# Attention weights transposed by VectorE and DRAM, with TensorE's and the transfers' order fixed by a timetable, in a two-layer graph kernel

## The chip, the cores and the metric

One core of one Trainium2 chip. Times are device microseconds (us) of the whole kernel, all in float32. A kernel is timed beside the kernel before on the same chip in alternating rounds. "The kernel before" took 3456.9 us (median of 4 runs in the rounds with the change, 3453.3 to 3458.0).

## The reference, cut to what matters

There are 128 graphs of 128 nodes with 256 features, and a dense integer adjacency (values 0 and 1) per graph. Layer 0 is two rounds of graph attention, a residual, a layer norm and a feed-forward block. Layer 1 is attention with 8 heads whose weights are masked by relation before they meet the values:

```python
# layer 0, twice:
e = leaky_relu(Wh1 + swapaxes(Wh2, 1, 2)); att = softmax(where(adj > 0, e, NEG), axis=1); h = att @ Wh
# layer 1:
attn = softmax(q @ k.T / sqrt(dh))                       # 8 heads, 128 x 128 each
for r in range(4):
    out += (attn * (adj == r)) @ (src @ Wv[r] + bv[r])   # needs attn with the nodes j on partitions
x = ln(src + out @ Wo + bo); x = ln(x + gelu(x @ W1) @ W2)
```

The last matmul contracts over `j`, so the attention weights, which come out of the softmax with `i` on partitions, have to be transposed: 8 blocks of 128x128 per graph, 1024 in all.

## The kernel before

It works on groups of four graphs, 32 groups, in five stages (load, graph attention, feed-forward 0, attention, feed-forward 1) that overlap between groups. The parts that the change touches:

```python
def transposed(y, direct):                 # of activations: VectorE turns 32x32 blocks, DRAM moves them
    ...
    nc.vector.transpose(z, y)
    for i in range(NQ):                    # four writes of 128 KB, runs of 128 bytes
        nc.sync.dma_start(s[:, :, i]..., z[ts(i, Q)]...)
    nc.sync.dma_start(t, s...)             # one read of 512 KB

def gat_weighting(wh, c, cap, direct):     # graph attention's weights
    nc.vector.transpose(z, wh[:, :, c + 1:c + 2].to_broadcast([P, G, Q]))
    nc.sync.dma_start(s..., z[::Q])        # the row transfer: 2 KB out ...
    nc.sync.dma_start(p, ...)              # ... and 256 KB back, the same row on all partitions
    # ScalarE, VectorE, ScalarE, GpSimd -> att

def by_relation(b, es):                    # attention: TensorE transposes, VectorE masks from PSUM
    for e in es:
        pT = ps.tile([P, HC, N], F32, name="tr", bufs=2)
        for q in range(HC):
            nc.tensor.transpose(pT[:, q], e[:, q], ident)                             # line 369
        for r in range(R):
            nc.vector.scalar_tensor_tensor(m, ab, r, pT, op0=OP.is_equal, op1=OP.mult)  # line 373
...
with tile.TileContext(nc, schedule_with_timeline_sim=True) as tc:
```

The stages are generators; a heap steps them by a virtual time, which sets priorities. The final order of every engine's instructions, and of the transfers in the one issuing queue, comes from a simulated timeline. It is fixed when the kernel is built.

Of the kernel before, what the change touches and what calls it, by code (L numbers as in the profile page):

```python
# [23 lines left out]
G = 4  # L24
Q = 32
# [14 lines left out]
def graph_layers(ctx: ExitStack, tc: tile.TileContext, a: dict, out: bass.AP):  # L40
# [21 lines left out]
    TB, KB = 4, 6  # L62
# [6 lines left out]
    ps = ctx.enter_context(tc.tile_pool(name="ps", bufs=5, space=PSUM))  # L69
# [69 lines left out]
    plus = wk.tile([P, 3, D], F32, name="plus", tag="T", bufs=TB)  # L139
# [72 lines left out]
    def transposed(y, direct):  # L212

        t = wk.tile([P, G, DC, N], F32, name="T", bufs=TB)
        if direct:
            for c in range(DC):
                p = ps.tile([P, G, N], F32, name="tr", bufs=2)
                for b in range(G):
                    nc.tensor.transpose(p[:, b], y[:, b, ts(c, P)], ident)
                if c % 2:  # L220
                    nc.vector.tensor_copy(t[:, :, c], p)
                else:
                    nc.scalar.copy(t[:, :, c], p)
            return t
        z = wk.tile([P, G, D // Q, Q], F32, name="z", bufs=1)
        nc.vector.transpose(z, y)  # L226
        s = dr.tile([G, D, NQ, Q], F32, name="zd")
        for i in range(NQ):
            nc.sync.dma_start(s[:, :, i].rearrange("b (j a) t -> a (b j) t", a=Q),
                              z[ts(i, Q)].rearrange("a b j t -> a (b j) t"))  # L230
        nc.sync.dma_start(t, s.rearrange("b (c p) i t -> p b c (i t)", p=P))
        return t

    def feed_forward(y, before, direct, win, bin_, wout, func, by=G):


        hT = transposed(y, direct)
        yield 2
        fT = []
        for f0 in range(0, FC, 2):  # L240
# [8 lines left out]
            yield 1  # L249
            if f0 in (2, 4):  # L250
                affine(y, before, f0 - 2)
        for b2_ in range(0, G, 2):
# [5 lines left out]
            yield 2  # L258
# [4 lines left out]
    def gat_weighting(wh, c, cap, direct):  # L263

        e = wk.tile([P, G, N], F32, name="e")
        if direct:
            p = ps.tile([P, G, N], F32, name="tr", bufs=2)
            for b in range(G):
                nc.tensor.transpose(p[:, b], wh[:, b, c + 1:c + 2].to_broadcast([P, N]), ident)
        else:  # L270
# [4 lines left out]
            p = wk.tile([P, G, N], F32, name="row", bufs=1)  # L275
# [13 lines left out]
    def gat_block(direct, xg, xt, at):  # L289
# [3 lines left out]
        wh = wk.tile([P, G, MW], F32, name="wh", tag="wh", bufs=1)  # L293
        for b in range(G):
# [4 lines left out]
            if b % 2:  # L299
                yield 1  # L300
        att = gat_weighting(wh, D + 2, cap, direct)
        yield 6
        wh2 = wk.tile([P, G, D + 2], F32, name="wh2", bufs=1)
        for b in range(G):
            p = ps.tile([P, D + 2], F32, name="mm")
            nc.tensor.matmul(p, att[:, b], wh[:, b, :D + 2], start=True, stop=True)  # L306
            nc.scalar.copy(wh2[:, b], p)
        yield 1
        att = gat_weighting(wh2, D, cap, direct)
        yield 6  # L310
        y = xg
        for b2_ in range(0, G, 2):
            p = ps.tile([P, 2, D], F32, name="mm")
            for b in (b2_, b2_ + 1):
                nc.tensor.matmul(p[:, b - b2_], att[:, b], wh2[:, b, :D], start=True, stop=True)  # L315
# [4 lines left out]
    def attention(y, at, direct):  # L320

        hT = transposed(y, direct)
        yield 2
        qT = wk.tile([P, DC, T], F32, name="T", bufs=TB)
# [13 lines left out]

        def weights(b):
# [8 lines left out]
            es = []  # L348
            for p in scores:
# [4 lines left out]
                e = wk.tile([P, HC, N], F32, name="e1", bufs=4)  # L354
                for q in range(HC):
                    nc.scalar.activation(e[:, q], p[:, q], AF.Exp, bias=nm[:, q:q + 1], accum_out=s[:, q:q + 1])  # L356
                nc.vector.reciprocal(s, s)  # L357
                nc.gpsimd.tensor_mul(e, e, per_row(s, N))  # L358
                es.append(e)
            return es  # L360

        def by_relation(b, es):

            ab = at[:, b][:, None, :].to_broadcast([P, HC, N])
            ms = []
            for e in es:
                pT = ps.tile([P, HC, N], F32, name="tr", bufs=2)
                for q in range(HC):
                    nc.tensor.transpose(pT[:, q], e[:, q], ident)  # L369
                ms.append([])  # L370
                for r in range(R):
                    m = wk.tile([P, HC, N], F32, name="m", bufs=DC * R)
                    nc.vector.scalar_tensor_tensor(m, ab, r, pT, op0=OP.is_equal, op1=OP.mult)  # L373
# [27 lines left out]
        yield 1  # L401
        es = [weights(0)]
        yield 1
        es.append(weights(1))
        yield 1
        for b in range(G):
# [3 lines left out]
            v = values(b)  # L410
            yield 1.5

            with tc.high_priority(offset=200):
                oT, last = weighted(ms, v)
                if b + 2 < G:
                    with tc.issue_after(last.ins):
                        es.append(weights(b + 2))
            yield 1.5
# [3 lines left out]
            nc.vector.tensor_add(y[:, b], y[:, b], p)  # L422
        normalised(y)
# [19 lines left out]
    def stage_gat(g):  # L443
        x0[g], masks[g] = yield from gat_block(g < 2, *loads.pop(g))
# [8 lines left out]
    def stage_attention(g):  # L453
# [5 lines left out]
        x2[g] = yield from attention(x1.pop(g), masks.pop(g), alone(g))  # L459

    def stage_ff1(g):
# [6 lines left out]
        if not last:  # L468
            nc.sync.dma_start(out[g], y)

    stages = ((stage_load, 1, -0.8, -0.7000000000000001), (stage_gat, 15, -0.1, 0.45), (stage_ff0, 9, 0.7, 1.2),
              (stage_attention, 17, 1.7, 3), (stage_ff1, 9, 3.2, 3.7))
    todo = []
    for g in range(NG):
        for n, (stage, total, begin, end) in enumerate(stages):
            if g == 1 and n == 1:
                begin, end = begin - 0.6, end - 0.6
            todo.append([g + begin, n, g, stage(g), (end - begin) / total])
    heapq.heapify(todo)
    while todo:  # L480
        t, n, g, steps, each = heapq.heappop(todo)
        try:
            share = next(steps)
        except StopIteration:
# [52 lines left out]
```

## Time and profile before

| | kernel before |
|---|---|
| time | 3456.9 us |
| TensorE busy | 98% of the span, 95% of the chain that ended last |
| other engines | at most 51% (ScalarE) |
| DMA | 20.8% of 16 engines |
| distance of line 306 in successive groups ("the period") | 104.0 us |

The period is read from start times in the trace: the mean over 20 groups in the middle. The middle of the kernel, 1000 to 2800 us, is the place to look. In the view of stretches the columns are the stretch, its length, then busy time and number of instructions of TensorE, its weight load, VectorE, ScalarE and GpSimd, then the granted clock (of TensorE; 1.00 is full speed), the DMA's share and GB/s. Line numbers are those of each kernel's own file: line 319 of the changed kernel is 306 before, and 321 in the runs that hold the masks back. Of before:

```profile
1000.00:2800.00 1800.00, 1800.00 (x10514) 1170.61 (x10513) 892.03 (x1944) 954.79 (x2530) 640.00 (x732) 1.00 0.23 54
```

TensorE has no idle time here. (Some matmul records are missing from any trace, so counts between traces are not compared.)

### The profile page before, as it was taken

The page shows a single profiled execution, that of the slowest core. Times are in us where ns is not written, and L with a number is a line of the kernel's source. Part 1 is how long each engine was busy: PE and PEld are TensorE (multiplying, and loading weights), DVE is VectorE, ACT ScalarE, POOL GpSimd, SP SyncE. Part 2 cuts the span into 40 slices and gives each one's busy share as a digit, 9 for nine tenths or more (in the row PEclk, how much of TensorE's full clock was granted, in tenths as well). Part 3 has the DMA queues.
Part 4 walks back from the last instruction along what each step waited for, and adds up shares of the span by engine and source line. Part 5 has one row for each costly group of instructions (what it writes and reads, how often), then busy time and mean ns, then how long its engine had stood idle before and what let it go on. Part 6 is the DMA issues. An engine that isn't in the chain of part 4 may idle for free.

```text
span 3451.6 us, 51872 instructions
## 1 busy us (share of the span) xinstructions
PE 3381.2 (98%) x19624; PEld 2197.9 (64%) x19624; DVE 1655.4 (48%) x3605; ACT 1763.8 (51%) x4724; POOL 1176.5 (34%) x1352
## 2 busy tenths in 40 slices
PE   7999999999999999999999999999999999999987
PEld 5656666666666666666666666666666666666655
DVE  2544454544454544454444454444454444554443
ACT  3444555645545645546545556545556545556332
POOL 2233343233333333333333333333333333333332
PEclk9999999999999999999999999999999999999999
DMA  5012222122222122221222221222221222221000
GB/s 188 13 41 55 57 47 55 47 65 51 60 47 52 50 62 53 56 52 47 55 62 53 56 53 44 59 62 53 56 53 42 60 62 53 49 44 38 19 19 13
DMA packets 501769, 181.10 MB, mean 52 GB/s; under 512 B 380432, under 2 KB 476176, under 8 KB 501392
## 3 DMA queue, kind: packets, MB, share of 16 engines
q1 hardware_dynamic: 501520, 177.79, 20.8%
q8 instruction: 155, 2.54, 0.3%
q14 instruction: 94, 0.77, 0.1%
HBM read 113.66 MB, written 64.09 MB: 51 GB/s over the span
## 4 chain that ended last, share of the span: by engine, by line
PE 95%; DVE 2%; ACT 1%; DMA 1%; POOL 0%; SPq 0%; issue 0%; ACTq 0%; DVEq 0%; POOLq 0%
PE mm L256 26%; PE mm L244 26%; PE mm L382 12%; PE av L394 7%; PE mm L346 5%; PE mm L297 4%; PE tr L369 3%; PE mm L334 3%; PE mm L328 3%; PE mm L421 3%; PE mm L306 2%; PE mm L315 2%; DVE m L373 1%; PE mm L172 0%; DMA zd<-z 0%; DMA wf<-in_wf_dram 0%
## 5 line engine op out<-in xcount | busy, mean ns | idle before, releaser
L210 POOL TENSOR_TENSOR tok<-tok,ln_rows 128x512 f32<-128x512 f32 x508 | 630.4, 1273 | 334.1 <-DVE z L226 172.8
L358 POOL TENSOR_TENSOR e<-e,s 128x512 f32<-128x512 f32 x256 | 266.3, 1041 | 1209.3 <-DVE s L357 983.3
L373 DVE SCALAR_TENSOR_TENSOR m<-at,tr 128x512 f32<-128x512 int32 x1024 | 629.6, 680 | 99.5 <-PE av L394 64.0
L247 ACT ACTIVATE fT<-mm,col 128x512 f32<-128x512 f32 x512 | 342.9, 691 | 415.1 <-PE mm L244 412.8
L244 PE MATMUL mm<-T,w 128*128 128x512 f32 x1024 | 471.6, 599 | 7.3 <-DMA T<-zd 5.4
L244 PE MATMUL mm<-T,wf 128*128 128x512 f32 x1024 | 466.5, 599 | 5.3 <-DMA T<-zd 3.7
L256 PE MATMUL mm<-w,fT 128*128 128x256 f32 x2048 | 470.6, 381 | 0.0
L382 PE MATMUL mm<-wv,T 128*128 128x512 f32 x1024 | 467.5, 594 | 0.0
L256 PE MATMUL mm<-wf,fT 128*128 128x256 f32 x2048 | 453.4, 379 | 0.0
L256 PEld LDWEIGHTS mm<-w,fT 128*128 128x128 f32 x2048 | 386.5, 190 | 97.9 <-issue 44.6
L256 PEld LDWEIGHTS mm<-wf,fT 128*128 128x128 f32 x2048 | 388.1, 191 | 66.2 <-issue 16.5
L352 DVE TENSOR_REDUCE nm<-mm 128x4 f32<-128x512 f32 x256 | 166.2, 681 | 541.8 <-PE mm L346 541.8
L204 ACT ACTIVATE tok<-tok,nmr,rstd 128x256 f32<-128x256 f32 x512 | 268.7, 590 | 259.8 <-POOL nmr L202 250.8
L398 ACT COPY oT<-av 128x256 f32<-128x256 f32 x128 | 47.9, 374 | 673.9 <-PE av L394 673.2
L356 ACT ACTIVATE e<-mm,nm 128x128 f32<-128x128 f32 x1024 | 359.8, 372 | 18.1 <-DVE nm L352 16.6
L244 PEld LDWEIGHTS mm<-T,wf 128*128 128x128 f32 x1024 | 196.3, 192 | 225.8 <-issue 209.2
L244 PEld LDWEIGHTS mm<-T,w 128*128 128x128 f32 x1024 | 188.1, 191 | 208.1 <-issue 190.3
L382 PEld LDWEIGHTS mm<-wv,T 128*128 128x128 f32 x1024 | 192.4, 191 | 176.1 <-issue 166.4
L394 PEld LDWEIGHTS av<-m,v 128*32 128x32 f32 x8192 | 217.1, 110 | 72.8 <-issue 44.6
L394 PE MATMUL av<-m,v 128*32 128x128 f32 x8192 | 251.8, 275 | 10.0 <-DVE v L383 8.8
L257 DVE TENSOR_TENSOR tok<-tok,mm 128x512 f32<-128x512 f32 x128 | 86.6, 676 | 319.8 <-PE mm L256 309.1
L337 ACT ACTIVATE kbd<-mm,col 32x512 f32<-32x512 f32 x256 | 173.9, 679 | 85.6 <-PE mm L334 83.0
(84 smaller groups left out, 3667.7 us busy)
## 6 DMA issues: line engine op xcount, KB each, us to landing
zd<-z SPq DMA_DIRECT2D x360, 128.0 KB
T<-zd SPq DMA_DIRECT2D x90, 512.0 KB
xt<-in_xT_dram SPq DMA_DIRECT2D x32, 512.0 KB
tok<-in_x_dram SPq DMA_DIRECT2D x32, 512.0 KB
out_dram<-tok SPq DMA_DIRECT2D x31, 512.0 KB
row<-zsd SPq DMA_DIRECT2D x60, 256.0 KB
at<-in_adjT_dram SPq DMA_DIRECT2D x32, 256.0 KB
wf<-in_wf_dram SPq DMA_DIRECT2D x2, 1024.0 KB
```

What stands on the lines that cost most here:

```text
L204: nc.scalar.activation(y[:, b], y[:, b], AF.Identity, bias=nmr[:, b:b + 1], scale=rstd[:, b:b + 1])
L210: engine.tensor_tensor(y[:, b:b + 2], y[:, b:b + 2], v[:, None, :].to_broadcast([P, 2, D]), op)
L244: nc.tensor.matmul(p, win[:, c, ts(f0 + i, P)], hT[:, :, c], start=c == 0, stop=c == DC - 1)
L247: nc.scalar.activation(t, p, func, bias=bin_[:, f0 + i:f0 + i + 1])
L256: nc.tensor.matmul(p[:, b - b2_], fT[f][:, ts(b, N)], wout[:, f], start=f == 0, stop=f == FC - 1)
L337: nc.scalar.activation(kbd[c][rows, :, q % 2], p[rows], AF.Identity, bias=bk[rows, c:c + 1])
L346: nc.tensor.matmul(scores[h][:, c], qT[rows, c, ts(b, N)], kbd[c][rows, b], start=True, stop=True, tile_position=(h * P // 2, 0))
L356: nc.scalar.activation(e[:, q], p[:, q], AF.Exp, bias=nm[:, q:q + 1], accum_out=s[:, q:q + 1])
L358: nc.gpsimd.tensor_mul(e, e, per_row(s, N))
L373: nc.vector.scalar_tensor_tensor(m, ab, r, pT, op0=OP.is_equal, op1=OP.mult)
L382: nc.tensor.matmul(p, hT[:, b, f], wv[:, f, r:r + 2], start=f == 0, stop=f == DC - 1)
L394: last = nc.tensor.matmul(po[ts(q, DH), c], v[:, r, c * P + q * DH:c * P + (q + 1) * DH], ms[q // 2][r][:, c * 2 + q % 2], start=r == R - ...
```

## The change

Two things. First, the attention weights of 31 of the 32 groups are transposed as activations already were: VectorE turns blocks in place, four writes to DRAM and a read put them together (`eT`). That is meant to free TensorE. Second, latency is planned by a timetable in units of about a microsecond per stage step, 100 units per group, and TensorE and the issuing queue (SP) are made to keep the order in which the program emits instructions. VectorE, ScalarE and GpSimd still get theirs from the simulated timeline. Smaller things come with it: one more PSUM bank for matmuls (in this program, the piece of memory that matmuls write a result into and that another engine reads before it is used again), a copy of the adjacency into PSUM, the values of a graph computed one step ahead, and no raised priority any more for the small matmuls with the attention weights.

```diff
+KEPT = {mybir.EngineType.PE: (250, 3150), mybir.EngineType.SP: (0, 4000)}
...
-    ps = ctx.enter_context(tc.tile_pool(name="ps", bufs=5, space=PSUM))
+    ps = ctx.enter_context(tc.tile_pool(name="ps", bufs=6, space=PSUM))
...  (gat_weighting: steps of the stage, in units)
-        yield 6
+        yield 29
...  (attention)
+        adj = ps.tile([P, G, N], F32, name="adj", bufs=1)
+        nc.vector.tensor_copy(adj, at)
...
-            return es
+            return e if direct else turned(e)
+        def turned(e):
+            eT = wk.tile([P, H, N], F32, name="eT")
+            transposed(e, eT, direct, over=True)
+            return eT
...  (by_relation)
-                pT = ps.tile([P, HC, N], F32, name="tr", bufs=2)
-                for q in range(HC):
-                    nc.tensor.transpose(pT[:, q], e[:, q], ident)
-                    nc.vector.scalar_tensor_tensor(m, ab, r, pT, op0=OP.is_equal, op1=OP.mult)
+                    nc.vector.scalar_tensor_tensor(m, ab, r, eT[:, ts(h, HC)], op0=OP.is_equal, op1=OP.mult)
...
+    stages = (stage_load, -75), (stage_gat, -31), (stage_ff0, 40), (stage_attention, 125), (stage_ff1, 290)
...  (for every new instruction i of an engine in KEPT)
+                tc.add_manual_dep(i, last[i.engine], ... NoSync ..., reason="order of emission")
```

More of the change, by code (lines that the diff above doesn't have):

```diff
@@ L24 @@
 G = 4
+LEAD = 35
+EARLY = {(1, 1): 70, (1,2): 50, (2,0): 80, (2,1): 90, (2,2): 90}
+KEPT = {mybir.EngineType.PE: (250, 3150), mybir.EngineType.SP: (0, 4000)}
 Q = 32
@@ L61, in graph_layers @@
     HC = P // DH
-    TB, KB = 4, 6
+    TB, KB = 5, 6
     SCALE = 1.0 / float(np.sqrt(DH))
@@ L138, in graph_layers @@
     nc.sync.dma_start(ln_rows, on_all_rows(0, 8))
-    plus = wk.tile([P, 3, D], F32, name="plus", tag="T", bufs=TB)
+    plus = wk.tile([P, G * MW], F32, name="plus", tag="T", bufs=TB)[:, :3 * D].rearrange("p (k d) -> p k d", k=3)
     nc.sync.dma_start(plus, on_all_rows(8, 3))
@@ L210, in affine, with transposed, t_tile, features @@
             engine.tensor_tensor(y[:, b:b + 2], y[:, b:b + 2], v[:, None, :].to_broadcast([P, 2, D]), op)
-    def transposed(y, direct):
-        t = wk.tile([P, G, DC, N], F32, name="T", bufs=TB)
+    def transposed(y, t, direct, over=False):
+        n = y.shape[1]
         if direct:
-            for c in range(DC):
-                p = ps.tile([P, G, N], F32, name="tr", bufs=2)
+            for k in range(0, n, G):
+                p = ps.tile([P, G, N], F32, name="mm")
                 for b in range(G):
-                    nc.tensor.transpose(p[:, b], y[:, b, ts(c, P)], ident)
-                if c % 2:
-                    nc.vector.tensor_copy(t[:, :, c], p)
-                else:
-                    nc.scalar.copy(t[:, :, c], p)
-            return t
-        z = wk.tile([P, G, D // Q, Q], F32, name="z", bufs=1)
+                    nc.tensor.transpose(p[:, b], y[:, k + b], ident)
+                if k:
+                    nc.vector.tensor_copy(t[:, k:k + G], p)
+                else:
+                    nc.scalar.copy(t[:, k:k + G], p)
+            return
+        z = y if over else wk.tile([P, n, N], F32, name="z", bufs=1)
         nc.vector.transpose(z, y)
-        s = dr.tile([G, D, NQ, Q], F32, name="zd")
+        s = dr.tile([n, N, NQ, Q], F32, name="zd", bufs=8)
         for i in range(NQ):
-            nc.sync.dma_start(s[:, :, i].rearrange("b (j a) t -> a (b j) t", a=Q),
-                              z[ts(i, Q)].rearrange("a b j t -> a (b j) t"))
-        nc.sync.dma_start(t, s.rearrange("b (c p) i t -> p b c (i t)", p=P))
+            nc.sync.dma_start(s[:, :, i].rearrange("k (j a) t -> a (k j) t", a=Q),
+                              z[ts(i, Q)].rearrange("a k (j t) -> a (k j) t", t=Q))
+        nc.sync.dma_start(t, s.rearrange("k p i t -> p k (i t)"))
+    def t_tile():
+        return wk.tile([P, G * MW], F32, name="T", bufs=TB)[:, :G * D]
+    def features(y, direct):
+        t = t_tile().rearrange("p (b c n) -> p b c n", b=G, c=DC)
+        transposed(y.rearrange("p b (c f) -> p (b c) f", f=P), t.rearrange("p b c n -> p (b c) n"), direct)
         return t
     def feed_forward(y, before, direct, win, bin_, wout, func, by=G):
-        hT = transposed(y, direct)
-        yield 2
+        hT = features(y, direct)
+        yield LEAD
         fT = []
@@ L248, in feed_forward @@
                 fT.append(t)
-            yield 1
+            yield 6
             if f0 in (2, 4):
@@ L257, in feed_forward @@
             nc.vector.tensor_add(y[:, b2_:b2_ + 2], y[:, b2_:b2_ + 2], p)
-            yield 2
+            yield 12.5
             if (b2_ + 2) % by == 0:
@@ L266, in gat_weighting @@
         if direct:
-            p = ps.tile([P, G, N], F32, name="tr", bufs=2)
+            p = ps.tile([P, G, N], F32, name="mm")
             for b in range(G):
@@ L274, in gat_weighting @@
             nc.sync.dma_start(s.rearrange("b i t -> i b t"), z[::Q])
-            p = wk.tile([P, G, N], F32, name="row", bufs=1)
+            p = e
             nc.sync.dma_start(p, bass.AP(tensor=s.tensor, offset=s.offset, ap=[[0, P], [1, G * N]]))
@@ L287, in gat_weighting, with gat_block @@
         return e
-    def gat_block(direct, xg, xt, at):
+    def gat_block(direct, tag, xg, xt, at):
         cap = wk.tile([P, G, N], F32, name="cap")
         nc.vector.tensor_scalar(cap, at, 0, 2 * BIG, op0=OP.is_gt, op1=OP.mult)
-        wh = wk.tile([P, G, MW], F32, name="wh", tag="wh", bufs=1)
+        wh = wk.tile([P, G, MW], F32, name="wh", tag=tag, bufs=TB if tag == "T" else 1)
         for b in range(G):
@@ L299, in gat_block @@
             if b % 2:
-                yield 1
+                yield 3
         att = gat_weighting(wh, D + 2, cap, direct)
-        yield 6
-        wh2 = wk.tile([P, G, D + 2], F32, name="wh2", bufs=1)
+        yield 29
         for b in range(G):
@@ L306, in gat_block @@
             nc.tensor.matmul(p, att[:, b], wh[:, b, :D + 2], start=True, stop=True)
-            nc.scalar.copy(wh2[:, b], p)
-        yield 1
-        att = gat_weighting(wh2, D, cap, direct)
-        yield 6
+            nc.scalar.copy(wh[:, b, :D + 2], p)
+        yield 2
+        att = gat_weighting(wh, D, cap, direct)
+        yield 29
         y = xg
@@ L314, in gat_block @@
             for b in (b2_, b2_ + 1):
-                nc.tensor.matmul(p[:, b - b2_], att[:, b], wh2[:, b, :D], start=True, stop=True)
+                nc.tensor.matmul(p[:, b - b2_], att[:, b], wh[:, b, :D], start=True, stop=True)
             nc.vector.tensor_add(y[:, b2_:b2_ + 2], xg[:, b2_:b2_ + 2], p)
@@ L318, in gat_block, with attention @@
         return y, at
-    def attention(y, at, direct):
-        hT = transposed(y, direct)
-        yield 2
-        qT = wk.tile([P, DC, T], F32, name="T", bufs=TB)
+    def attention(y, at, first, direct):
+        hT = features(y, first or direct)
+        yield LEAD
+        qT = t_tile().rearrange("p (c t) -> p c t", c=DC)
         for c in range(DC):
@@ L347, in weights @@
                                      start=True, stop=True, tile_position=(h * P // 2, 0))
-            es = []
-            for p in scores:
+            e = wk.tile([P, H, N], F32, name="e1")
+            for h, p in enumerate(scores):
                 p = p.rearrange("p c q n -> p (c q) n")
@@ L353, in weights, with by_relation @@
                 s = sm.tile([P, HC], F32, name="s1")
-                e = wk.tile([P, HC, N], F32, name="e1", bufs=4)
+                eh = e[:, ts(h, HC)]
                 for q in range(HC):
-                    nc.scalar.activation(e[:, q], p[:, q], AF.Exp, bias=nm[:, q:q + 1], accum_out=s[:, q:q + 1])
+                    nc.scalar.activation(eh[:, q], p[:, q], AF.Exp, bias=nm[:, q:q + 1], accum_out=s[:, q:q + 1])
                 nc.vector.reciprocal(s, s)
-                nc.gpsimd.tensor_mul(e, e, per_row(s, N))
-                es.append(e)
-            return es
-        def by_relation(b, es):
-            ab = at[:, b][:, None, :].to_broadcast([P, HC, N])
+                nc.gpsimd.tensor_mul(eh, eh, per_row(s, N))
+            return e if direct else turned(e)
[3 more added lines that the diff above has]
+            return eT
+        def by_relation(b, eT):
+            if direct:
+                eT = turned(eT)
+            ab = adj[:, b][:, None, :].to_broadcast([P, HC, N])
             ms = []
-            for e in es:
-                pT = ps.tile([P, HC, N], F32, name="tr", bufs=2)
-                for q in range(HC):
-                    nc.tensor.transpose(pT[:, q], e[:, q], ident)
+            for h in range(2):
                 ms.append([])
@@ L399, in weighted @@
             return oT, last
-        yield 1
+        yield 7
         es = [weights(0)]
-        yield 1
+        yield 5
         es.append(weights(1))
-        yield 1
+        yield 24
+        v = values(0)
         for b in range(G):
@@ L409, in attention @@
             ms = by_relation(b, es.pop(0))
-            v = values(b)
-            yield 1.5
-            with tc.high_priority(offset=200):
-                oT, last = weighted(ms, v)
-                if b + 2 < G:
-                    with tc.issue_after(last.ins):
-                        es.append(weights(b + 2))
-            yield 1.5
+            yield 10
+            oT, last = weighted(ms, v)
+            if b + 2 < G:
+                es.append(weights(b + 2))
+            yield 5
+            if b + 1 < G:
+                v = values(b + 1)
+            yield 4
             p = ps.tile([P, D], F32, name="mm")
@@ L422, in attention @@
             nc.vector.tensor_add(y[:, b], y[:, b], p)
+            if b + 1 < G:
+                yield 6
         normalised(y)
@@ L443, in stage_gat @@
     def stage_gat(g):
-        x0[g], masks[g] = yield from gat_block(g < 2, *loads.pop(g))
+        x0[g], masks[g] = yield from gat_block(g < 2, "T" if g == 1 else "wh", *loads.pop(g))
     def alone(g):
@@ L458, in stage_attention @@
             folded(w1, b1, "11")
-        x2[g] = yield from attention(x1.pop(g), masks.pop(g), alone(g))
+        x2[g] = yield from attention(x1.pop(g), masks.pop(g), g == 0, g == NG - 1)
     def stage_ff1(g):
@@ L469, in stage_ff1 @@
             nc.sync.dma_start(out[g], y)
-    stages = ((stage_load, 1, -0.8, -0.7000000000000001), (stage_gat, 15, -0.1, 0.45), (stage_ff0, 9, 0.7, 1.2),
-              (stage_attention, 17, 1.7, 3), (stage_ff1, 9, 3.2, 3.7))
+    stages = (stage_load, -75), (stage_gat, -31), (stage_ff0, 40), (stage_attention, 125), (stage_ff1, 290)
     todo = []
     for g in range(NG):
-        for n, (stage, total, begin, end) in enumerate(stages):
-            if g == 1 and n == 1:
-                begin, end = begin - 0.6, end - 0.6
-            todo.append([g + begin, n, g, stage(g), (end - begin) / total])
+        for n, (stage, begin) in enumerate(stages):
+            todo.append([100 * g + begin - EARLY.get((g, n), 0), n, g, stage(g)])
     heapq.heapify(todo)
+    traced = nc.cur_bb.bb.instructions
+    last = {}
     while todo:
-        t, n, g, steps, each = heapq.heappop(todo)
-        try:
-            share = next(steps)
-        except StopIteration:
-            continue
-        heapq.heappush(todo, [t + share * each, n, g, steps, each])
+        t, n, g, steps = heapq.heappop(todo)
+        before = traced[-1]
+        step = next(steps, None)
+        new = []
+        for i in reversed(traced):
+            if i is before:
+                break
+            new.append(i)
+        for i in reversed(new):
+            if i.engine not in KEPT:
+                continue
+            if i.engine in last and KEPT[i.engine][0] <= t <= KEPT[i.engine][1]:
+                tc.add_manual_dep(i, last[i.engine], mybir.DependencyInfo(
+                    mybir.DependencyClass.NoSync, mybir.DependencyReason.DATA), reason="order of emission")
+            last[i.engine] = i.name
+        if step is not None:
+            heapq.heappush(todo, [t + step, n, g, steps])
 def by_group(x):
```

## The prediction

> **What bounds the kernel now.** I read the page first, then the stretches by time, the costliest groups, the chain of work in order of time in one stretch, the timeline of TensorE, and the timeline of the DMA-issuing queue. The page's shares and the chain that ended last:
>
> ```profile
> PE 3381.2 (98%) x19624; PEld 2197.9 (64%) x19624; DVE 1655.4 (48%) x3605; ACT 1763.8 (51%) x4724; POOL 1176.5 (34%) x1352
> ...
> PE 95%; DVE 2%; ACT 1%; DMA 1%; POOL 0%; SPq 0%; issue 0%; ACTq 0%; DVEq 0%; POOLq 0%
> ```
>
> TensorE is busy 98% of the span and is 95% of the chain; no other engine passes 51%. The stretches show where it is not:
>
> ```profile
> 0.00:60.00 60.00, 37.47 (x128) 29.68 (x128) 14.98 (x34) 20.04 (x70) 9.13 (x17) 0.89 0.69 252
> ...
> 110.00:210.00 100.00, 87.90 (x532) 54.26 (x531) 47.63 (x100) 42.27 (x134) 23.80 (x26) 0.95 0.16 35
> ...
> 1600.00:2200.00 600.00, 600.00 (x3490) 386.80 (x3489) 295.21 (x644) 322.62 (x845) 209.49 (x237) 1.00 0.22 54
> ...
> 3340.00:3452.00 112.00, 85.44 (x468) 54.24 (x464) 32.83 (x73) 28.47 (x67) 21.86 (x30) 0.90 0.06 17
> ```
>
> From 400 to 2800 us every microsecond is TensorE's (600.00 of 600.00); idle time lies in the first 210 us and the last 112. Any time saved must come out of TensorE's own stream. The starts of line 306 in successive groups of four graphs are 104.0 us apart, the same to 0.1 us for over 25 groups, so the span is about 31 x 104.0 = 3224 us plus 228 us of start and end.
>
> Busy time misleads about one group, because matmuls overlap. The transposes of the attention weights (line 369):
>
> ```profile
> L369 PE MATMUL tr<-ident,e 128*128 128x128 f32 x1024 | 156.4, 277 | 3.2 <-DVE m L373 2.8 <-POOL e L358 0.4
> ```
>
> 156.4 us is an upper bound. In the chain by order of time, where each piece is only what it adds, eight of them, then four matmuls of line 421 and eight of line 382, read:
>
> ```profile
> 1644.41 0.87 PE tr L369 x8
> 1645.28 0.87 PE mm L421 x4
> 1646.15 3.43 PE mm L382 x8
> ```
>
> So one transpose costs 0.87/8 = 0.109 us of TensorE. Taking start-to-next-start over 400 to 2800 us (23 groups), line 369 holds 87.3 us, that is **3.80 us per group** of 32 transposes (0.119 each; some are followed by a switch that costs a little). The chain's 3% for line 369 (about 104 us) agrees.
>
> **What the Trainium skill says.** "Trainium Kernel Development and Optimization", Performance Expectations: matmul busy time is a bad metric of the distance to roofline, since matmuls are pipelined. This trace agrees: 277 ns mean against 109 ns added. "TensorE: Matmul & The Clock Gate", Part 4, calls a TensorE transpose a matmul against the identity with its result in PSUM, about 275 ns in one kernel; the duration here is 277. "VectorE: DVE Perf Modes", The three transpose paths, says that VectorE's transpose makes a grid of separately turned 32x32 blocks; so the kernel must move blocks by four writes to DRAM and a read, which it already does for activations (line 226). "SBUF — State Buffer" says that VectorE and GpSimd exclude each other on a shared port pair when a VectorE instruction has two SBUF inputs; that fits the new copy of the adjacency into PSUM, which leaves the masking with one SBUF input as before. The trace of before does not show such a lock for line 373, which reads one PSUM operand.
>
> **The change, part by part.**
>
> Removed from TensorE: the 32 transposes per group, in 31 of 32 groups (the last keeps them): 31 x 3.80 = **118 us**; at the bare 0.109, 108 us.
>
> Added to VectorE: one 128x1024 transpose per graph, 124 in all, by the same instruction's row:
>
> ```profile
> L226 DVE STREAM_TRANSPOSE z<-tok 128x1024 f32<-128x1024 f32 x90 | 112.0, 1245 | 205.4 <-DMA zd<-z 136.4 <-ACT tok L204 66.3
> ```
>
> 124 x 1.245 = 154 us, and 32 copies of the adjacency to PSUM at about 0.69 (like line 221), 22 us. VectorE goes from 1655 to about 1831 us, 55% of a shorter span: beside TensorE's work. The masking (line 373, 0.680 us each) has swapped operands but the same size; I keep its time.
>
> Added to the DMA: 124 x 5 transfers. In the trace one such transpose has 4096 packets of 128 bytes at 13.1 ns and 1024 of 512 bytes at 28.6 ns, together 83 us of one engine, 5.2 us of all sixteen. 124 x 5.2 = 645 us over some 3340: the DMA share rises from 0.21 to about 0.4. The traffic grows by 130 MB. The issuing queue:
>
> ```profile
> 2047.55 2.66 SPq L229 DMA_DIRECT2D zd<-z  x4
> 2052.71 0.38 SPq L231 DMA_DIRECT2D T<-zd  x1
> 2054.05 3.68 SPq L229 DMA_DIRECT2D zd<-z  x4
> 2060.16 0.38 SPq L231 DMA_DIRECT2D T<-zd  x1
> ```
>
> 5.2 us from the first write to the read, 6.6 us of queue time per transpose. Seven per group instead of three make 46 us, with the rest some 55 of 100: it fits, but the queue is in order. The read lands about 4 us after its issue: one issued at 3342.9 let TensorE start at 3346.94.
>
> Moved: transposes now stand between softmax and masking. From the scores on: two reductions 1.4, eight exponentials 8 x 0.58 = 4.7, reciprocals 0.3, two multiplications by GpSimd 2.1, the transpose 1.2, DRAM 5.2 + 4.4, eight maskings 5.4: about 25 us (estimate from the rows). The timetable has 100 units per group and leaves from the scores to their use 5+24+10 = 39 units for the first graph and 50 for the third and fourth. A unit is close to 1 us, so some 14 us are spare: hidden, unless the queue is blocked. TensorE's order is now the timetable's in the middle; before it was that of a simulated timeline. The stream was full before and should be full again, so I give the order itself no gain. One more PSUM bank for matmuls is neutral.
>
> Sum: period 104.0 - 3.8 = 100.2 us. 31 x 100.2 + 228 = 3334 us of span; times are some 6 us above the profiled span. I predict **3338 us** (-3.5%).
>
> **The rivals.**
>
> (a) **A wait takes the transposes' place.** Transfers are issued strictly in order. The output transfer is queued in the step that starts its normalisation, and waits for ScalarE and GpSimd (about 14 us from the rows). Behind it stands the row transfer of the graph attention, with 29 units until TensorE needs its result. If this or a late transposed tile stops TensorE 2 us per group, 62 us are lost: 3400 us. For it: the queue is over half full and in order. Against: margins of 29 to 50 units against paths of 12 to 25 us.
>
> (b) **The start and the end grow.** The first group's weights go through DRAM while little other work exists, and the attention stage is 165 units long where it was 130. That may cost 10 to 40 us once: 3350 to 3380. Against: groups 1 and 2 are started 50 to 90 units early, and the last group keeps TensorE transposes.
>
> (c) **The stream gets tighter.** The sum of bare durations (0.429 us per 512 columns, 0.216 per 256, 1.89 per 64 small ones) is 98.0 us per group without transposes; 100.2 holds 2.2 us of switches and small stalls. If the timetable saves half: 3300 us. For it: fewer switches, and two banks no longer reserved for transposes. Against: switches between tiled and whole matmuls remain.
>
> (d) **VectorE or DMA becomes the bound.** At 55% and about 40% I think not; then the gain would vanish: 3450 or more.
>
> **Range and chances.** (a) and (b) push up, (c) down: 3295 to 3390 should hold it eight times in ten. Two per cent faster is 3389, so the range's upper end lies there: 0.89 faster, 0.09 within 2%, 0.02 slower.
>
> **What would show it.** Line 369 at 32 instead of 1024 instructions; TensorE still full in 600-us stretches; line 306 about 100.2 us apart; 214 VectorE transposes of 1.25 us; DMA near 0.4. A distance over 102 us with TensorE waiting for a transfer shows (a); more idle in the first 250 or last 120 us shows (b); a distance under 99 shows (c). I would be wrong above all by a repeated queue stall that no row of before can show.

## The result, and the profile after

The change is **slower**: 3590.5 us (median of 4, 3581.0 to 3591.1) against 3456.9. The ratio is 1.038, with a 95% interval of 1.036 to 1.040. A ratio here is the mean time of one kernel's runs over that of the other's of the same rounds, so it is not quite the ratio of the medians quoted. The prediction was 3338 us with a range of 3295 to 3390; it was wrong in size and in direction.

The page of the changed kernel, its shares and its chain of work:

```profile
PE 3333.5 (93%) x18632; PEld 2109.8 (59%) x18632; DVE 1841.7 (51%) x3765; ACT 1602.3 (45%) x4614; POOL 1188.9 (33%) x1352
...
PE 40%; DVE 19%; DMA 16%; POOL 10%; ACT 6%; SPq 4%; issue 3%; POOLq 0%; DVEq 0%; ACTq 0%
```

TensorE has 992 matmuls fewer, as intended. But its part of the chain fell from 95% to 40%: TensorE no longer sets the time, and no other engine took its place as a busy one. The time goes through a loop of VectorE, transfers, GpSimd and ScalarE. The stretch in the middle, of after:

```profile
1000.00:2800.00 1800.00, 1703.69 (x9584) 1073.77 (x9585) 955.69 (x1949) 829.71 (x2388) 615.76 (x694) 0.97 0.41 91
```

TensorE is idle 96.3 of 1800 us, and its granted clock is 0.97 where it was 1.00. The period grew from 104.0 to 108.2 us, where 100.2 was expected. Idle time is 96.3/1800 x 108.2 = 5.8 us of a period. The lower clock costs, as an estimate, 0.03 x (108.2 - 5.8) = 3.1 us. Without both, 99.3 us would be left. That is about the predicted period, and some 9 us per group came on top of it as waits and clock.

The waits of TensorE in the changed kernel, longest first (total us, times, longest):

```profile
PE mm L319 <- POOL e L300: 131.2, 31, 13.4
PE mm L258 <- DVE tok L329: 54.6, 29, 3.2
```

Both come once in each group. In the kernel before, the longest such total was 9.1 us. The first is the graph attention's first matmul (line 319), which waits for its weights. Three views of one period show why. TensorE:

```profile
1968.21 7.07 PE L270 MATMUL mm<-wf,fT 128*128 128x256 f32 x32
1979.25 3.44 PE L319 MATMUL mm<-wh,e 128*128 128x258 f32 x8 [3.96 <-POOL e L300]
```

VectorE makes the row for the row transfer (line 286):

```profile
1950.91 0.29 DVE L286 STREAM_TRANSPOSE zs<-wh 128x128 f32<-128x128 f32 x1
```

And the issuing queue:

```profile
1950.44 2.64 SPq L235 DMA_DIRECT2D zd<-e  x4
1955.60 0.38 SPq L237 DMA_DIRECT2D eT<-zd  x1
1957.37 3.22 SPq L235 DMA_DIRECT2D zd<-e  x4
1963.09 0.38 SPq L237 DMA_DIRECT2D eT<-zd  x1
1963.52 0.57 SPq L491 DMA_DIRECT2D out_dram<-tok  x1
1964.13 0.54 SPq L288 DMA_DIRECT2D zsd<-zs  x1
1969.21 0.33 SPq L290 DMA_DIRECT2D e<-zsd  x1
```

The row was ready at 1951.20, and its 2 KB were issued at 1964.13: they stood 12.9 us behind two transposed weights and the output. Then they took another 5 us to land. TensorE, which may not take anything else first, stood still for 4 us. What follows is slow as well: the eight matmuls of line 319 took 3.44 us, where the same eight (line 306 in the kernel before) took 2.01. The granted clock from 1979.66 to 1983.07 us was 0.50. The Trainium skill, "TensorE: Matmul & The Clock Gate", Part 1, says that the clock goes to half after an idle window of about 3.4 us. The half clock after this stand agrees with it in kind, but a shorter stand was enough elsewhere in this kernel. The line below shows one of 2.44 us: the eight matmuls after it took 5.32 us, where eight of that line mostly take 3.60 to 3.70. There are three such cases at line 258 between 1000 and 2800 us, of 2.07 to 2.44 us. (The ends of matmuls are modelled, so a stand's length is not exact.)

```profile
1365.38 5.32 PE L258 MATMUL mm<-T,w 128*128 128x512 f32 x8 [2.44 <-DVE tok L329]
```

The second wait (line 258, for the add of line 329) is about VectorE. The matmul needs a PSUM bank, which the graph attention's final add frees. VectorE at that time, in the changed kernel:

```profile
2005.90 2.48 DVE L392 SCALAR_TENSOR_TENSOR m<-adj,eT 128x512 f32<-128x512 f32 x4 [7.54 <-DMA eT<-zd]
2008.30 1.24 DVE L232 STREAM_TRANSPOSE z<-tok 128x1024 f32<-128x1024 f32 x1
2009.46 2.44 DVE L392 SCALAR_TENSOR_TENSOR m<-adj,eT 128x512 f32<-128x512 f32 x4
2011.83 0.58 DVE L306 TENSOR_SCALAR cap<-at 128x512 f32<-128x512 int32 x1
2012.33 1.28 DVE L368 TENSOR_REDUCE nm<-mm 128x4 f32<-128x512 f32 x2
2013.52 1.27 DVE L329 TENSOR_TENSOR tok<-tok,mm 128x512 f32<-128x512 f32 x2
```

VectorE stood 7.5 us for a transposed tile at the head of its own queue, masked it, and only then did the score reductions and the add. The skill's "TensorE: Matmul & The Clock Gate", in the table at its top, calls VectorE's queue strict FIFO; this trace agrees, for the add was ready and stood. That masking is not needed until 2030 us; the add was needed at 2012.4, when TensorE ran out of banks.

### The profile page after: what moved, and what is told of

Read it like the earlier page. It is cut to its first block, busy times and chain, and to the rows that moved or that the text cites. A ratio compares the mean times of both kernels' runs of the same rounds, so it can differ in the third digit from the quotient of the medians.

```text
span 3589.3 us, 50735 instructions
## 1 busy us (share of the span) xinstructions
PE 3333.5 (93%) x18632; PEld 2109.8 (59%) x18632; DVE 1841.7 (51%) x3765; ACT 1602.3 (45%) x4614; POOL 1188.9 (33%) x1352
## 4 chain that ended last, share of the span: by engine, by line
PE 40%; DVE 19%; DMA 16%; POOL 10%; ACT 6%; SPq 4%; issue 3%; POOLq 0%; DVEq 0%; ACTq 0%
PE mm L270 13%; DVE m L392 7%; DMA zd<-e 6%; POOL e L374 5%; DMA zsd<-zs 4%; PE mm L258 4%; PE mm L401 4%; PE av L413 4%; DMA eT<-zd 3%; SPq L235 3%; PE mm L311 3%; POOL tok L214 3%; PE mm L341 3%; PE mm L319 3%; PE mm L347 3%
## 5 line engine op out<-in xcount | busy, mean ns | idle before, releaser
L392 DVE SCALAR_TENSOR_TENSOR m<-adj,eT 128x512 f32<-128x512 f32 x1024 | 629.6, 679 | 353.6 <-DMA eT<-zd 285.5
L214 POOL TENSOR_TENSOR tok<-tok,ln_rows 128x512 f32<-128x512 f32 x508 | 645.6, 1302 | 495.9 <-DVE z L232 478.7
L258 PE MATMUL mm<-T,w 128*128 128x512 f32 x1024 | 474.6, 607 | 55.5 <-DVE tok L329 54.6
L202 POOL TENSOR_SCALAR rstd<-mv 128x4 f32<-128x4 f32 x129 | 30.0, 233 | 1241.9 <-DVE mv L200 1239.3
L413 PEld LDWEIGHTS av<-m,v 128*32 128x32 f32 x8192 | 232.9, 116 | 98.3 <-issue 84.1
L413 PE MATMUL av<-m,v 128*32 128x128 f32 x8192 | 273.6, 288 | 14.6 <-DVE mv L200 6.9
L372 ACT ACTIVATION_READ_ACCUMULATOR e<-mm,nm 128x1 f32 x1024 | 239.5, 234 | 0.0
```

What stands on the lines that cost most here:

```text
L214: engine.tensor_tensor(y[:, b:b + 2], y[:, b:b + 2], v[:, None, :].to_broadcast([P, 2, D]), op)
L258: nc.tensor.matmul(p, win[:, c, ts(f0 + i, P)], hT[:, :, c], start=c == 0, stop=c == DC - 1)
L372: nc.scalar.activation(eh[:, q], p[:, q], AF.Exp, bias=nm[:, q:q + 1], accum_out=s[:, q:q + 1])
L392: nc.vector.scalar_tensor_tensor(m, ab, r, eT[:, ts(h, HC)], op0=OP.is_equal, op1=OP.mult)
L413: last = nc.tensor.matmul(po[ts(q, DH), c], v[:, r, c * P + q * DH:c * P + (q + 1) * DH], ms[q // 2][r][:, c * 2 + q % 2], start=r == R - ...
```

## The experiments

The theories: **Q**, the kept order of the transfers blocks a small, urgent one. **V**, VectorE's order, left to the simulated timeline, blocks behind a late tile. **P**, TensorE's kept order is what costs. **D**, the transposes through DRAM as such, their load and latency, cost. Times are medians; ratios are to the kernel before in the same rounds.

### One kept order at a time: sp_free, pe_free, both_free

```diff
-KEPT = {mybir.EngineType.PE: (250, 3150), mybir.EngineType.SP: (0, 4000)}
+KEPT = {mybir.EngineType.PE: (250, 3150)}     # sp_free
+KEPT = {mybir.EngineType.SP: (0, 4000)}       # pe_free
+KEPT = {}                                     # both_free
```

> The changed kernel with the issuing queue's order left to the simulated timeline again; TensorE's order stays the timetable's. Theory Q (the recurring loss comes from the fixed order of the transfers: the graph attention's row transfer stands behind both transposed-weight transfers and the output transfer, TensorE then waits about 4 us per group at line 319): 3330 to 3430 us, the wait at line 319 falls from 131 us to under 40. Theory P (the fixed order of TensorE costs the time, as it cannot go round a late tile): stays at 3560 to 3600. Theory D (the transposes through DRAM as such, their load and latency): stays at 3560 to 3600.

> The changed kernel with TensorE's order left to the simulated timeline; the issuing queue's order stays the timetable's. Theory P: 3330 to 3430 us, the waits of TensorE go. Theory Q: 3540 to 3620 us, as the row transfer is as late as before. Theory D: 3560 to 3600.

> The changed kernel with both orders left to the simulated timeline: the transposes through DRAM alone, with the new start times only as priorities. Theory D: 3560 us or more. Theories Q and P: 3330 to 3450 us, unless the simulated timeline, which does not know the real latencies, makes waits of its own.

Measured: sp_free 3535.8 us (ratio 1.023), pe_free 3561.1 (1.030), both_free 3537.0 (1.024). No theory got its number. In sp_free the wait at line 319 did go, from 131.2 to 10.9 us, as Q says. But the other wait grew:

```profile
PE mm L258 <- DVE tok L329: 150.1, 28, 6.5
...
PE mm L319 <- POOL e L300: 10.9, 2, 5.9
```

So one wait stood in for the other: a loop with two blocked places does not get much shorter when one is opened. P alone is out, since pe_free kept the waits (50.3 us at line 319, 63.1 at the add). With both orders free the add's wait was still 86.6 us. What all of these share is VectorE's order, or D.

### The timetable with TensorE's transposes: pe_turns

```diff
-        x2[g] = yield from attention(x1.pop(g), masks.pop(g), g == 0, g == NG - 1)
+        x2[g] = yield from attention(x1.pop(g), masks.pop(g), g == 0 or g == NG - 1, True)
-        hT = features(y, first or direct)
+        hT = features(y, first)
```

> The timetable alone: both orders kept, but the attention weights of all groups transposed by TensorE again (992 transposes more, at 0.109 to 0.119 us, with copies by ScalarE and VectorE out of PSUM). Period by sums: 98.0 + 3.5 and switches, 102 to 104 us. Theories Q and D: the queue has only the old transfers, so the row transfer is in time: 3430 to 3500 us with no wait of more than 1 us per group at line 319. Theory P: 3560 us or more, as the order is still fixed.

Measured: 3539.8 us (1.025). The wait at line 319 was 10.9 us in all, as Q and D say for an unburdened queue, but the time missed their range. It made a wait of its own: the last matmuls waited 89.9 us for the masking, because transposing, copying out of PSUM and masking all fell into the 10 units ahead of their use. (That they fall there is read from the program.) The run does not isolate the timetable and settles nothing about D.

### VectorE's order: mask_late and mask_late_sp_free

The masking may not come, on VectorE, before the last emitted add of the graph attention. This is an order without a wait between engines; no transfer, size or buffer changes.

```diff
-                    nc.vector.scalar_tensor_tensor(m, ab, r, eT[:, ts(h, HC)], op0=OP.is_equal, op1=OP.mult)
+                    mask = nc.vector.scalar_tensor_tensor(m, ab, r, eT[:, ts(h, HC)], op0=OP.is_equal, op1=OP.mult)
+                    if gat_added:
+                        tc.add_manual_dep(mask.ins, gat_added[0], ... NoSync ...)
```

mask_late_sp_free also has the queue's order free, as in sp_free.

> The changed kernel with one thing added: VectorE may not mask an attention weight before the last emitted adds of the graph attention's result. Theory V (VectorE's own order, left to the simulated timeline, puts the masking that waits for the transposed tile ahead of the add that frees a matmul's PSUM bank; TensorE then waits in line 258): TensorE's wait for that add falls from 54.6 us to under 5; the wait at line 319 stays at 100 to 140 us; 3490 to 3560 us. Rival B (the bank wait is only where TensorE's slack shows, the transfer's latency bounds the loop): the wait moves to another line and the time stays within 15 us of 3590.

> The same, and the issuing queue's order left to the simulated timeline. Theories Q and V together: both waits go (line 319 was 10.9 us with the free queue, the add's wait 150.1 us), the granted clock comes back to 0.99, the period is 99 to 102 us: 3310 to 3410 us. Rival B: 3500 us or more.

Measured: mask_late 3573.1 us (1.034), mask_late_sp_free **3340.5 us (0.967**, 0.966 to 0.969). In mask_late the add's wait is gone from the list, but the time hardly fell, against V's number. The wait moved, as rival B said (whose number, within 15 us of 3590, it missed by 2):

```profile
PE mm L321 <- POOL e L300: 124.4, 31, 13.2
PE mm L407 <- ACT e L375: 57.6, 27, 3.4
```

The first is still the graph attention's weights. The second is for exponentials, whose score reductions on VectorE now stood behind another late transfer (see below). With the queue freed as well, the middle closes:

```profile
1000.00:2800.00 1800.00, 1791.77 (x10394) 1148.50 (x10392) 1025.29 (x2119) 898.87 (x2608) 660.43 (x761) 1.00 0.45 98
```

The clock is back at 1.00 and the period is 99.75 us. With the queue free, the hold on the masks is worth 3535.8 - 3340.5 = 195 us; with the queue kept, 17 us. Freeing the queue without the hold is worth 55 us; both together 250. (The simulated timeline places all other instructions of VectorE, ScalarE and GpSimd anew in each run; what part of the 195 us is that was not separated.) Theory D is out: the same 124 transposes through DRAM, with a DMA share of 0.45, run beside a full TensorE.

### Moving the row transfer in the timetable: gat_early and mask_late_gat_early

```diff
-    stages = (stage_load, -75), (stage_gat, -31), (stage_ff0, 40), (stage_attention, 125), (stage_ff1, 290)
+    stages = (stage_load, -75), (stage_gat, -41), (stage_ff0, 40), (stage_attention, 125), (stage_ff1, 290)
```

> The changed kernel with the graph attention's stage 10 units earlier in the timetable, so that the row transfer stands before both transposed-weight transfers and the output transfer in the kept order; VectorE's order free as in the change. Theory Q: the wait at line 319 falls from 131 us to under 30; theory V: the add's wait stays or grows (30 to 150 us); 3400 to 3550 us together. If line 319's wait stays, theory Q is wrong.

> Both: the row transfer first and the masking after the add, with both orders kept. Theories Q and V: 3310 to 3400 us, TensorE full in the middle, granted clock 0.99 or more. Rival B: 3500 us or more.

Measured: 3561.5 us (1.031) and 3561.8 us (1.031). The first wait fell to about 11 us in both, as Q says, and the times missed. With the graph attention earlier, its second row transfer was the late one (90.0 us waited at line 328 in gat_early; in one period its row was ready at 1955.55 us and issued at 1965.85), and matmuls waited 80.4 us for banks that the exponentials had yet to read. Moving one stage by 10 units moved the blocked place; it did not remove it. Here the hold on the masks changed nothing.

### Taking the row transfers out of the line: mask_late_row_act

```diff
-            nc.sync.dma_start(s.rearrange("b i t -> i b t"), z[::Q])
+            nc.scalar.dma_start(s.rearrange("b i t -> i b t"), z[::Q])
...
-            nc.sync.dma_start(p, bass.AP(tensor=s.tensor, ...))
+            nc.scalar.dma_start(p, bass.AP(tensor=s.tensor, ...))
```

on mask_late, both orders kept.

> Masks after the add, both orders kept, but the graph attention's two row transfers (2 KB out, 256 KB back) are issued from ScalarE's queue, so that they cannot stand behind a transposed weight. Theory Q (what hurts is this one transfer standing in line): the wait at line 321 falls from 124 us to under 30 and the time to 3310 to 3420 us. Rival Q2 (the fixed order of the queue hurts at many transfers, the row only being the first to show): another wait of 1.5 us per group or more appears and the time stays over 3480 us.

Measured: 3454.3 us (1.001, 0.999 to 1.002). Taking the two row transfers of each group (2 KB out and 256 KB back each) out of the line gave 119 us against mask_late, and the wait for the graph attention's weights fell from 124.4 to 11.2 us. That is Q, shown without touching the order of anything else in the queue. But the time fell between both theories' ranges, and another wait was left: 86.0 us in 27 waits for the exponentials. The issuing queue and VectorE in one such place:

```profile
2032.85 0.38 SPq L237 DMA_DIRECT2D eT<-zd  x1
2033.27 0.58 SPq L83 DMA_DIRECT2D xt<-in_xT_dram  x1
2033.89 0.43 SPq L85 DMA_DIRECT2D at<-in_adjT_dram  x1
```

```profile
2038.81 1.16 DVE L308 TENSOR_SCALAR cap<-at 128x512 f32<-128x512 int32 x1 [4.14 <-DMA at<-in_adjT_dram]
2039.88 1.27 DVE L371 TENSOR_REDUCE nm<-mm 128x4 f32<-128x512 f32 x2
```

The next group's adjacency load stood behind a transposed weight. VectorE waited 4.1 us for it in order to prepare a mask that nobody needed yet. Behind that stood the score reductions; behind those the exponentials and a PSUM bank; TensorE's next matmuls waited 3.1 us.

### Holding that preparation back too: mask_cap_late_row_act and mask_cap_late_sp_free

```diff
-        nc.vector.tensor_scalar(cap, at, 0, 2 * BIG, op0=OP.is_gt, op1=OP.mult)
+        capped = nc.vector.tensor_scalar(cap, at, 0, 2 * BIG, op0=OP.is_gt, op1=OP.mult)
+        if gat_added:
+            tc.add_manual_dep(capped.ins, gat_added[0], ... NoSync ...)
```

> Both orders kept, rows from ScalarE's queue, masks after the add, and now VectorE's mask preparation from the next adjacency (line 308) may not come before the last emitted add either. Theory Q3 (what was left at 3454 us is again VectorE standing at one late transfer, the adjacency load behind a transposed weight in the kept queue, 4.1 us each, with the score reductions and so a PSUM bank behind it): TensorE's wait on ScalarE's exponentials falls from 86 us to under 20, 3340 to 3400 us. Rival Q2 (the kept queue order is wrong at many places): a further wait appears and the time stays over 3420 us.

> The queue's order free, masks and preparation after the add. Beside the 3340 us of masks alone: the 12 us of waits on the exponentials go, 3315 to 3345 us. Also the timed candidate for a version that beats both.

Measured: mask_cap_late_row_act **3320.1 us (0.961**, 0.960 to 0.962), faster than the kernel before by 135 us and than the change by 270 us, with both of the change's kept orders still in place. The middle and the chain of this kernel:

```profile
1000.00:2800.00 1800.00, 1799.73 (x10481) 1155.95 (x10480) 1034.26 (x2127) 904.60 (x2635) 669.69 (x768) 1.00 0.45 99
```

```profile
PE 94%; DVE 2%; DMA 1%; ACT 1%; issue 0%; POOL 0%; SPq 0%; ACTq 0%; DVEq 0%; POOLq 0%
```

TensorE is full at full clock; the period is 99.1 us. The time came out below the 3340 to 3400 expected of Q3 (VectorE standing at one more late transfer). Q3 holds, and Q2 (the kept order wrong at many places) falls: two changes of VectorE's order and the row transfers on another queue repair the change. mask_cap_late_sp_free took 3344.2 us (0.968), no better than masks alone in the free order (3340.5), where VectorE stood 1.8 us in all for an adjacency, against 136.7 us in mask_late_row_act. It lies in its expected range, but the 12 us of waits for exponentials that were to go stayed (13.6 us).

### What TensorE's kept order is worth: mask_late_both_free

> Masks after the add, and both orders left to the simulated timeline. Tells what TensorE's kept order is worth. If nothing, as the prediction said: 3320 to 3360 us, within 20 us of the 3340 with TensorE's order kept. If TensorE's own order costs (theory P): under 3320. If the kept order is a gain: over 3360.

The edit is mask_late with `KEPT = {}`. Measured: 3400.0 us (0.984), period 102.0 us, against 3340.5 and 99.75 with TensorE's order kept and the queue free in both. So for the changed work TensorE's kept order is worth 60 us against the simulated timeline's. In the stretch 1000 to 2200 us TensorE is "busy" throughout in both:

```profile
1000.00:2200.00 1200.00, 1200.00 (x6833) 745.95 (x6833) 669.82 (x1378) 589.03 (x1704) 426.03 (x492) 1.00 0.44 96
```

The difference is inside busy time. Between 1000 and 2800 us the small tiled matmuls (line 419) switched to another line 213 times in this kernel and 72 times with the kept order, and they held 36 against 29 ns each from start to start; over the 256 of a group that is 1.8 of the 2.2 us. Here the simulated timeline cuts blocks of 64 small matmuls into pieces, and the kept order leaves them whole. It did not cut them in the kernel before: there the same stretch has 69 switches, at 29 ns each. That kernel gave these blocks a raised priority, which the change left out; that this is the cause was not tested.

### How much is the transposes alone: fixed_pe_turns

On mask_late_sp_free, the edits of pe_turns, and the transposing moved ahead:

```diff
-            if direct:
-                eT = turned(eT)
...
+                if direct:
+                    es[0] = turned(es[0])      # with values(b + 1), 10 units ahead of use
```

> Masks after the add, the queue's order free, TensorE's kept, but TensorE makes the transposes of the attention weights, 10 units ahead of their use, with copies out of PSUM. Tells what part of the 3340 us comes from taking the transposes off TensorE: by the prediction's sum 31 x 3.5 to 3.8 us, so 3440 to 3480 us, period 103.2 to 104.0. If the timetable alone were the gain, it would stay below 3400 us.

Measured: 3530.4 us (1.022), period 106.3 us, over the expected range. Matmuls of line 270 waited 69.8 us for exponentials, and transposes held 718 ns on average where another line followed, mostly by waiting. This is again a kernel with its own blocked places, so it does not give the value of the transposes in isolation.

## Why the prediction was wrong, point by point

**What held.** TensorE bound the kernel before, and the added work was sized rightly. VectorE's total came to 1841.7 us (predicted 1831). The added transposes took 1.245 us each and the masking 0.679, as taken from before. The DMA share is 0.41 (about 0.4). The period of an unblocked kernel is 99.1 to 99.8 us (100.2), and the predicted 3338 us is met by mask_late_sp_free at 3340.5, a kernel with one more order on VectorE and the transfers' order left free. (The prediction's last sum has a slip without weight: 3334 and 6 are 3340.)

**The step that failed** is "some 14 us are spare: hidden, unless the queue is blocked". The path was compared with its own margin only, and its own margin was enough: the tile of the wait shown above landed at 2005.8 us, and TensorE used it at 2030. What was not compared is what stands behind the path's instructions in each in-order line. The queue was blocked, for the row transfer and for the adjacency load. And a tile in time for its user was late for its place in VectorE's line. Rival (a) named the wait at the graph attention's weights and its cause in the queue, but with the output transfer as the culprit, a size of 2 us per group, and too little weight; it named a late transposed tile too, but as one that stops TensorE, not VectorE. The trace shows two transposed weights as the main part of the 12.9 us stood, and about 9 us lost per group.

**VectorE "beside TensorE's work"** was the part nobody looked behind. At 51% it is not short of time, but it takes its work in order, and four PSUM-freeing or score-reading instructions stood behind a masking that stood for a transfer. The prediction treated VectorE's share as the test. Holding the masks back took no work away and gave 195 us once the queue was free (17 us before). Why the simulated timeline put the masking there was not measured; that it expects the transfers to land earlier than they do is inferred from the places where VectorE stood.

**"I give the order itself no gain"** failed for the queue, whose kept order cost. For TensorE it is nearly right, if it is read against the kernel before, as the prediction meant it. The 60 us of mask_late_both_free are a loss that the simulated timeline would have brought to the changed work, mostly by cutting blocks that were whole before. From start to next start in the middle, the way from 104.0 to the 99.75 us of mask_late_sp_free is: transposes 3.8 us, the 32 score matmuls of a group 1.1 us (133 ns each for 166; the same in mask_late_both_free, so not by the kept order), and back come 0.5 us of stands and 0.1 of the rest. So the transposes gave what was predicted, and the agreement of 99.75 with 100.2 is luck only in so far as a gain of 1.1 and a loss of 0.6 us, neither in the sum, partly cancel. The 99.1 us of mask_cap_late_row_act, without stands, are in size what rival (c) gave for a saving of half of the 2.2 us. In pe_turns, with both orders kept, the transposes hold 118 ns each, 3.8 us per group, as before. A kernel without waits that shows this difference in its whole time is lacking, as neither run with TensorE's transposes was free of them.

**The clock** was not in the sum. Stands of 2 to 5 us drew the granted clock to 0.97, by the estimate above 3 of the 9 us per group: between 1000 and 2800 us the record has 19 stretches of 3.4 or 6.8 us at half clock, 99 us together, each at a stand. No run separates it from the waits. In four kernels with a full or nearly full middle (before, mask_late_sp_free, mask_cap_late_row_act, mask_late_both_free) it was 1.00; but it was 1.00 in pe_turns too, where the stands in this stretch were no longer than 2.2 us (17 at line 413, one half-clock stretch), so not every wait draws it down.

Rival (d) did not come true: no engine and not the DMA became the bound. For rival (b), span less 31 periods is 228 us before and 235 after (3589.3 - 31 x 108.2), so start and end hardly grew. The copy of the adjacency into PSUM was not tested by itself.

## What to carry to other kernels

When work moves from a saturated engine to an idle engine and a transfer, check not only whether the new path is hidden for its own user, but which instructions stand behind it in every in-order line it passes, the issuing queue above all; an engine at half load can still stop the one that sets the time, through a PSUM bank it frees late. Put small urgent transfers in another line than large ones, and keep instructions that wait for transfers behind those that free buffers. When opening one blocked place moves the time little and a new wait appears, open the next one with the first still open before giving up on the cause.

## What the Trainium skill lacked or had wrong

- "TensorE: Matmul & The Clock Gate", Part 4, gives a transpose about 275 ns in one kernel. The mean duration here, in float32, is the same (277 ns), but in a stream of matmuls one adds 109 ns, 119 with its switches, which is the number to plan with; the page has none in a stream.
- The same page, Part 1, puts the half clock after an idle window of about 3.4 us. Here three stands of 2.07 to 2.44 us were followed by matmuls of 512 columns at 854 ns each for 429, with a granted clock of 0.50; one of 3.00 us was not. After the stand of 2.44 us the eight matmuls took at least 1.6 us more than their usual 3.60 to 3.70.
- "Perfetto Trace Analysis", Optimization Strategy, says that consistent bubbles can mean too little SBUF or PSUM. The bubble of up to 3.2 us per group at a PSUM bank here (54.6 us) was one of order: it went without another buffer, when the maskings moved behind the add on VectorE.
- No page tells of a small transfer's wait behind large ones in one issuing queue that waits for a landing between them: 12.9 us here for 2 KB, and 119 us of the kernel's time when the two row transfers of each group left the queue.
